# Where the first image's selective scan stands in the planner's order: in front of the scan inputs from its second direction on

## The chip, the core and the metric

The kernel runs on one core of one Trainium2 chip. The metric is device time in microseconds (us): the median of three runs before the change is 8721.23 us (8714.47 to 8724.86).

## What is computed

Four images of 64 x 64 tokens with 128 channels go through four layers: a Mamba-like block with a selective scan in four directions and an MLP (layer 0), a self attention over all 4096 tokens (layer 1), a block of convolutions (layer 2), and neighborhood attention with an MLP (layer 3). The change touches layer 0 alone. Cut to what matters there (DI = 256, N = 16, K = 4 directions, L = 4096):

```
xz = _ln(input) @ in_proj_w;  x_, z = split(xz)
xc = _silu(depthwise_conv3x3(x_) + conv_b)
xs = stack([x0, x1, x0 reversed, x1 reversed])      # row order, column order
dts, Bs, Cs = split(einsum(xs, x_proj_w))
delta = softplus(einsum(dts, dt_w) + dt_b)
h[t] = exp(delta[t] * A) * h[t-1] + (delta[t] * x[t]) * B[t]
y[t] = sum over N of h[t] * C[t]
y = the four directions added up, with Ds * xs
out = input + (_ln(y) * _silu(z)) @ out_proj_w;  then an MLP
```

## The kernel before

**The stages of an image.** `scan_inputs` (L283) makes what the scan reads: per chunk of 512 tokens the layer norm (its bn_stats and bn_aggr on VectorE, L194 and L196), the input projection, the 3 x 3 convolution on TensorE (L253), Silu on ScalarE, and then, in `steps` (L302), the projections to delta, B and C, softplus on ScalarE (L402, L403), and du = delta x xc on GpSimd (L334, two for each chunk and each order of tokens, 32 an image). All of it is stored to scratch memory: delta, B/C, sz and xc through ScalarE's queue (L331, L332, L388, L390), du through SyncE's (L338). The x loads stand on SyncE's queue too (L344). Each call opens its own pools, `si_a` and others, and closes them; the next pools that are opened lie on the same addresses and wait until the earlier ones are released.

`selective_scan` (L463) runs one image's scan: the four directions in the order 0, 1, 3, 2 (`ORDER`), eight chunks each, two halves of the channels, four groups of states and two pairs. One such step is called a unit here; an image has 512 units, 128 a direction. A unit is one product dB = du x B on GpSimd (L510), two exponentials dA on ScalarE (L516) and two scans on VectorE (L518), and then the product with C: on VectorE (L523), or, for 6 units of 16 of image 0 and 7 of 16 of the later images (`ON_POOL`), on GpSimd (L531). TensorE sums over the states (L564) into one PSUM tile `py`; ScalarE copies it out (L574, L581) and stores it. Directions 0 and 2 read what the token order by rows gives, 1 and 3 the order by columns. SyncE loads dt, du (L493), b_rows and c_rows (L503). The buffers: four each of dt, du, b_rows, c_rows and dB, three dA in PSUM, six hc.

`rest` (L1693) is everything behind the scan: `scan_output` (its weights are loaded first, w_onorm_w being the very first, then y, sz and x at L617 to L621), `layer1`, `layer2` and `layer3_attention` (last store at L1419). The layer 3 MLP of an image runs inside the next image's `scan_output`. `rest` opens its pools where those of `scan_inputs` lay.

**What sets the order.** The kernel is written in a tile framework. Each traced instruction takes a number from a running counter, `tc.cur_priority`. A planner plays the program through with its own durations and gives each engine, whenever that engine is free, the ready instruction with the lowest number; the order that comes out is fixed in the program. Waits between engines are semaphores. `network` (L1723) traces in this order: scan inputs of image 0, scan of image 0, `make_bias` (tables for layer 3), scan inputs of images 1 to 3, then, in turn, scan of image 1, rest of image 0, scan of image 2, rest of image 1, scan of image 3, rest of image 2, and rest of image 3. The scans are traced inside this block with a base of `SCAN_FIRST` = 10,000,000:

```
def priority(tc, K, base):
    kept = tc.cur_priority
    tc.cur_priority = K.next_priority.get(base, base)
    yield
    K.next_priority[base] = tc.cur_priority
    tc.cur_priority = kept
```

So a scan's numbers are above those of all scan inputs and rests: it takes what they leave. The groups of Silu and Gelu (`Together`, L101) have numbers of their own: the first of a group the highest (50 x `SCAN_FIRST`), the others and the return to the exp table the lowest (-100 x `SCAN_FIRST`).

After the scan inputs of image 3, `network` opens the pool `ss_more`, again on the addresses that scan inputs used, and calls `widen` (L452) for four more hc and one more dB tile. `Tiles.tile` (L455) counts from -40, so the first 40 tiles of image 1's scan still come from the old pool.

Of the kernel before, what the change touches and what calls it, by code (L numbers as in the profile page):

```python
# [53 lines left out]
ORDER = (0, 1, 3, 2)  # L54
BEHIND = 2
ON_POOL = ((1, 4, 6, 9, 12, 14), (0, 2, 4, 6, 9, 11, 13))
SCAN_FIRST = 10_000_000
# [20 lines left out]
@contextmanager  # L78
# [7 lines that stand above are left out]
# [42 lines left out]
def make_consts(ctx, tc):  # L128
    nc = tc.nc
    K = SimpleNamespace(next_priority={}, general=False)  # L130
    pool = ctx.enter_context(tc.tile_pool(name="consts", bufs=1))
    K.ident = pool.tile([128, 128], F32, name="ident")
    make_identity(nc, K.ident)
    K.ones = pool.tile([128, 128], F32, name="ones")
    nc.gpsimd.memset(K.ones, 1.0)
    K.mean_col = pool.tile([128, 1], F32, name="mean_col")
    nc.gpsimd.memset(K.mean_col, 1.0 / DI)
    K.mhalf = pool.tile([128, 128], F32, name="mhalf")
    nc.gpsimd.memset(K.mhalf, -0.5)
    K.half = pool.tile([128, 1], F32, name="half")  # L140
    nc.gpsimd.memset(K.half, 0.5)
    K.zeros = pool.tile([1, LC], mybir.dt.bfloat16, name="zeros")
    nc.gpsimd.memset(K.zeros, 0.0)
    K.eps = pool.tile([128, 1], F32, name="eps")
    nc.gpsimd.memset(K.eps, 1e-5)

    K.quads = pool.tile([128, 4], F32, name="quads")
    nc.gpsimd.memset(K.quads, 0.0)
    for r in range(4):
        nc.gpsimd.memset(K.quads[32 * r : 32 * r + 32, r : r + 1], 1.0)  # L150
        nc.gpsimd.memset(K.quads[32 * r : 32 * r + 1, :], 0.0)

    K.bounds = pool.tile([128, B, 8], F32, name="bounds")
    nc.gpsimd.memset(K.bounds, 0.0)

    K.first = pool.tile([128, 1], F32, name="first")
    K.first2 = pool.tile([128, 1], F32, name="first2")
    nc.gpsimd.memset(K.first, 0.0)  # L160
    nc.gpsimd.memset(K.first2, 0.0)
    for r in range(4):
        nc.gpsimd.memset(K.first[32 * r : 32 * r + 1, :], 1.0)
    for r in range(2):
        nc.gpsimd.memset(K.first2[64 * r : 64 * r + 1, :], 1.0)
    return K
# [104 lines left out]
def make_conv_diagonals(tc, K, A, out):  # L271
    nc = tc.nc
    with tc.tile_pool(name="mk_conv", bufs=1) as pool:
        convw = pool.tile([128, ND, 9], F32, name="convw")
        nc.sync.dma_start(convw, A["L0_conv_conv_w"])
        diag = pool.tile([128, ND, 9, 128], F32, name="conv_diag")
        for d in range(ND):
            for t in range(9):
                nc.scalar.activation(diag[:, d, t, :], K.ident, AF.Copy, scale=convw[:, d, t : t + 1])
        nc.sync.dma_start(out, diag)  # L280
# [135 lines left out]
def make_scan(ctx, tc, K, A):  # L416

    nc = tc.nc
    S = SimpleNamespace()
    big = ctx.enter_context(tc.tile_pool(name="ss_big", bufs=1))  # L420
    S.pool = ctx.enter_context(tc.tile_pool(name="ss", bufs=2))
    S.psum = ctx.enter_context(tc.tile_pool(name="ss_ps", bufs=1, space=PSUM))
    load = loader(tc, big, A, 0)
    S.A = load("A_log", [128, KD, NJS, NPR, 2])
    nc.scalar.activation(S.A, S.A, AF.Exp)
    nc.vector.tensor_scalar_mul(S.A, S.A, -1.0)
    ds4 = load("Ds", [128, ND, KD])
    total = big.tile([128, ND], F32, name="Dsum")
    nc.vector.tensor_reduce(total, ds4, AX.X, ALU.add)
    S.skip = big.tile([128, ND, 128], F32, name="skip_diag")  # L430
    for d in range(ND):
        nc.scalar.activation(S.skip[:, d, :], K.ident, AF.Copy, scale=total[:, d : d + 1])

    S.pick = big.tile([128, 32], F32, name="pick")
    nc.gpsimd.memset(S.pick, 1.0)
    for base, sign in ((0, 1), (3, -1)):
        nc.gpsimd.affine_select(
            S.pick, S.pick, [[-4 * sign, 32]], ALU.is_ge, 0.0, base=base, channel_multiplier=sign
        )
    S.unit = 0  # L440
    S.products = Tiles(S.pool, "hc", 6)
    S.inputs = Tiles(S.pool, "dB", 4)
    return S
# [16 lines left out]
        return pool.tile([128, 2, LC], F32, name=self.name, bufs=bufs)  # L460


def selective_scan(tc, K, S, D, img):  # L463

# [9 lines left out]
    def settle(unit):  # L476
        while waiting and waiting[0][0] <= unit:
            waiting.pop(0)[1]()

    for k in ORDER:  # L480
        back = k >= 2
        order = slice(None, None, -1) if back else slice(None)
        last = 0 if back else LC - 1
        state = pool.tile([128, NJS, NPR, 2], F32, name="state")
        for i in range(NCH):
            c = NCH - 1 - i if back else i
            for hf in range(2):
# [11 lines left out]
                for j in range(NJS):  # L499
# [85 lines left out]
                    waiting.append((max([S.unit] + [w[0] for w in waiting]), total))  # L585
                    settle(S.unit)
    settle(S.unit + BEHIND)


def scan_output(tc, K, A, D, img, xT, last, scan_over=None):  # L590
# [1132 lines left out]
def network(tc, A, out):  # L1723
    nc = tc.nc
    with ExitStack() as ctx:
        nc.scalar.preload_act_table_set("natural_log_exp_and_others")
        K = make_consts(ctx, tc)
        dram = ctx.enter_context(tc.tile_pool(name="scratch", bufs=1, space=DRAM))

        def scratch(name, shape):  # L1730
            return dram.tile(shape, F32, name=f"{name}_dram")

        D = SimpleNamespace()
        D.bias = scratch("bias", [len(BIAS_KINDS), 128, HEADS * 512])
        D.biasT = [[scratch(f"biasT{k}_{i}", [128, HEADS, LC]) for i in range(4)] for k in range(3)]
        D.T = scratch("T", [128, HEADS * (2 * KW - 1) + 1, W])
        D.conv_diag = scratch("conv_diag", [128, ND, 9, 128])
        D.w2_norms = scratch("w2_norms", [128, len(NORMS2), 4])
        D.w2_cv4, D.w2_bias = scratch("w2_cv4", [128, 128]), scratch("w2_bias", [1, 128])
        for name, shape in (("sz", [128, ND, LC]), ("xc", [128, ND, LC]), ("y", [128, ND, LC])):  # L1740
            setattr(D, name, [[scratch(f"{name}{b}_{c}", shape) for c in range(NCH)] for b in range(B)])
        for name, shape in (("delta", [128, ND, LC]), ("du", [128, ND, LC]), ("bc", [NS, 2, LC])):
            made = [
                [[scratch(f"{name}{b}_{k}_{c}", shape) for c in range(NCH)] for k in range(KD)] for b in range(B)
            ]
            setattr(D, name, made)
        D.y_first = [[[scratch(f"y_first{b}_{k}_{c}", [128, ND, LC]) for c in range(NCH)] for k in range(2)] for b in range(B)]
        D.y_cols = [scratch(f"y_cols{b}", [NCH, 128, NCH, ND, RC * RC]) for b in range(B)]
        for name in ("x4", "x5"):
            setattr(D, name, [scratch(f"{name}_{b}", [NT, C]) for b in range(B)])  # L1750
        D.shift = [scratch(f"shift{b}", [NJ, 128]) for b in range(B)]

        with ExitStack() as scan_ctx:
            S = make_scan(scan_ctx, tc, K, A)
            make_conv_diagonals(tc, K, A, D.conv_diag)
            with priority(tc, K, SCAN_FIRST // 2):
                with tc.tile_pool(name="mk_w2", bufs=1, side="right") as pool:
                    make_layer2(tc, K, A, D, pool)
            scan_inputs(tc, K, A, D, 0)
            before = None  # L1760
            for img in range(B):
                with priority(tc, K, SCAN_FIRST):
                    selective_scan(tc, K, S, D, img)
                if img == 0:
                    make_bias(tc, K, A, D)
                    for later in range(1, B):
                        scan_inputs(tc, K, A, D, later)
                    more = scan_ctx.enter_context(tc.tile_pool(name="ss_more", bufs=1))
                    S.products.widen(more, 4)
                    S.inputs.widen(more, 1)  # L1770
                else:
                    rest(tc, K, A, D, img - 1, before)
                    before = img - 1, out[img - 1]
            rest(tc, K, A, D, B - 1, before, scan_ctx.close, out[B - 1])
        needed = ctx.enter_context(tc.tile_pool(name="needed", bufs=1)).tile([1, 1], mybir.dt.int32, name="needed")
        bound_exceeded(tc, K, needed)
        with tc.If(nc.values_load(needed) > 0):
            everything_again(tc, K, A, D, out)
# [80 lines left out]
```

## Time and profile before

| what | us |
|---|---|
| median of three runs | 8721.23 |
| the profiled execution, its own time | 8724.62 |
| its span from first to last instruction | 8722.7 |
| scan inputs, first to last du product: image 0 | 79.8 to 518.7 |
| image 1 | 664.8 to 1080.7 |
| image 2 | 1166.3 to 1579.9 |
| image 3 | 1661.8 to 2084.6 |
| scan, start of the first and of the last dB product: image 0 | 101.2 to 2241.0 |
| image 1 | 2245.6 to 4049.3 |
| image 2 | 4053.9 to 5837.6 |
| image 3 | 5842.2 to 7640.4 |

The first three rows are read against each other: a sum that is made from the profile belongs to the span, and the execution that was profiled took 1.9 us more than its span. The du products show how far the scan inputs are, the dB products how far the scans are. In the profile's lines, PE is TensorE, PEld its weight loads, DVE is VectorE, ACT is ScalarE, POOL is GpSimd and SPq is SyncE's queue of DMA issues. L510 is line 510 of the kernel. A group of instructions is shown as out<-in, shapes and count, then its busy time and the mean of one in ns, then how long its engine was idle just before it and what ended that wait.

### The profile page before, as it was taken

How to read it: one execution, taken by the hardware profiler on the slowest of the kernel's cores; microseconds unless marked ns; L12 is line 12 of the kernel's file. 1: busy time of each engine (PE TensorE's matmuls, PEld its weight loads, DVE VectorE, ACT ScalarE, POOL GpSimd, SP SyncE). 2: the span in 40 equal slices, each digit the busy share in tenths (PEclk: the TensorE clock that was granted, in tenths of full speed). 3: DMA queues.
4: the chain of work that ended last, by engine and by line, in shares of the span. 5: the costliest groups of instructions: out<-in, count | busy, mean ns of one | idle time of the engine just before them, and what ended most of it. 6: DMA issues, size and time to landing. Idle time of an engine off the chain costs nothing. (4 is left out here: it accounts for less than half of the span.)

```text
span 8722.7 us, 102005 instructions
## 1 busy us (share of the span) xinstructions
PE 7011.5 (80%) x30532; PEld 2619.6 (30%) x30532; DVE 7102.0 (81%) x8456; ACT 5678.8 (65%) x11633; POOL 7121.9 (82%) x3111
## 2 busy tenths in 40 slices
PE   6858677686789987777899887777898877888988
PEld 2213122232422222233322222234322222344333
DVE  4788777778999999998899999998899999923433
ACT  5657676665666676667766676667766766654366
POOL 6899989999899989998899989998899999900000
PEclk8768687786899988888899988888999988899989
DMA  5676767677555556565555565565545565620020
GB/s 177 238 256 239 249 224 252 230 246 237 177 175 170 168 170 222 187 222 188 164 174 169 177 202 190 196 224 178 169 167 167 177 211 193 208 73 5 1 83 12
DMA packets 859600, 1562.74 MB, mean 179 GB/s; under 512 B 224389, under 2 KB 342300, under 8 KB 856733
## 3 DMA queue, kind: packets, MB, share of 16 engines
q1 hardware_dynamic: 728733, 1379.93, 48.2%
q10 hardware_dynamic: 130304, 176.19, 5.7%
q8 instruction: 245, 4.01, 0.2%
q14 instruction: 318, 2.61, 0.1%
HBM read 1286.50 MB, written 281.92 MB: 180 GB/s over the span
## 5 line engine op out<-in xcount | busy, mean ns | idle before, releaser
L510 POOL TENSOR_TENSOR dB<-du,b_rows 128x1024 f32<-128x1024 f32 x2048 | 4816.6, 2386 | 405.8 <-DVE hc L518 125.7
L516 ACT ACTIVATE dA<-dt,w_A_log 128x512 f32<-128x512 f32 x4096 | 2777.4, 690 | 482.3 <-DVE hc L518 257.7
L518 DVE TENSOR_TENSOR_SCAN dA<-dA,state,dB 128x512 f32<-128x512 f32 x2072 | 2563.4, 1274 | 289.8 <-POOL dB L510 151.8
L518 DVE TENSOR_TENSOR_SCAN hc<-dA,state,dB 128x512 f32<-128x512 f32 x1512 | 1874.1, 1270 | 303.3 <-ACT dA L516 114.2
L531 POOL TENSOR_TENSOR hc<-hc,c_rows 128x1024 f32<-128x1024 f32 x864 | 2061.9, 2386 | 60.6 <-ACT state L527 18.5
L523 DVE TENSOR_TENSOR hc<-dA,c_rows 128x512 f32<-128x512 f32 x2368 | 1526.0, 678 | 37.8 <-DMA c_rows<-bc_dram 15.2
L564 PE MATMUL py<-hc,pick 128*32 128x512 f32 x8192 | 1242.0, 681 | 266.6 <-POOL hc L531 230.9
L525 ACT COPY state<-dA 128x1 f32<-128x1 f32 x2072 | 319.2, 158 | 1225.5 <-DVE hc L523 1208.6
L854 PE MATMUL pa<-e,l_v 128*128 128x512 f32 x2048 | 1069.4, 654 | 14.9 <-ACT e L810 14.8
L810 ACT ACTIVATE e<-pair 128x1024 f32<-128x1024 f32 (+1 forms) x448 | 509.0, 1136 | 241.3 <-PE pair L806 233.7
L806 PE MATMUL pair<-l_g,l_f 32*128 32x512 f32 x2048 | 527.3, 662 | 169.6 <-ACT e L810 135.4
L854 PEld LDWEIGHTS pa<-e,l_v 128*128 128x128 f32 x2048 | 376.6, 200 | 667.1 <-issue 621.8
L994 POOL MEMSET l_h<- 64x128 f32 x8 | 1.9, 238 | 693.7 <-DVE l_h L968 693.7
L564 PEld LDWEIGHTS py<-hc,pick 128*32 128x32 f32 x8192 | 214.8, 116 | 1019.5 <-issue 476.1
L253 PE MATMUL ps<-band,w_conv_diag 128*128 128x504 f32 (+3 forms) x1152 | 499.0, 592 | 0.0
L1376 PE MATMUL pair<-table,ident 128*128 128x512 f32 x768 | 404.7, 652 | 104.2 <-ACT e L1386 68.7
L207 PE MATMUL ps<-ident,ln_xn 128*128 128x128 f32 x512 | 141.6, 375 | 377.4 <-ACT ln_xn L204 301.1
L518 DVE TENSOR_TENSOR_SCAN dA<-dA,dB 128x512 f32<-128x512 f32 x296 | 348.3, 1212 | 52.5 <-ACT dA L516 28.0
L334 POOL TENSOR_TENSOR du<-delta,xc 128x1024 f32<-128x1024 f32 x128 | 333.5, 2611 | 49.5 <-ACT delta L403 45.1
L1386 ACT ACTIVATE e<-pair 128x1024 f32<-128x1024 f32 (+1 forms) x224 | 254.3, 1135 | 101.4 <-PE pair L1380 100.7
L253 PEld LDWEIGHTS ps<-band,w_conv_diag 128*128 128x128 f32 x1152 | 220.3, 192 | 278.3 <-issue 259.7
L806 PEld LDWEIGHTS pair<-l_g,l_f 32*128 32x128 f32 x2048 | 138.4, 187 | 518.6 <-ACT e L810 266.9
(285 smaller groups left out, 8716.7 us busy)
## 6 DMA issues: line engine op xcount, KB each, us to landing
b_rows<-bc_dram SPq DMA_DIRECT2D x1024, 256.0 KB
c_rows<-bc_dram SPq DMA_DIRECT2D x1024, 256.0 KB
dt<-delta_dram SPq DMA_DIRECT2D x512, 512.0 KB
du<-du_dram SPq DMA_DIRECT2D x512, 512.0 KB
delta_dram<-delta ACTq DMA_DIRECT2D x128, 512.0 KB
du_dram<-du SPq DMA_DIRECT2D x128, 512.0 KB
table<-biasT_dram SPq DMA_DIRECT2D x72, 512.0 KB
y_first_dram<-y_sum ACTq DMA_DIRECT2D x128, 256.0 KB
```

What stands on the lines that cost most here:

```text
L253: mm = nc.tensor.matmul(out[:, r0 - row0 : r1 - row0, c0:c1], lhsT((dy + 1) * 3 + dx + 1), src[:, r0 + dy : r1 + dy, c0 + dx : c1 + dx], s ...
L334: nc.gpsimd.tensor_mul(du.rearrange("p d (a b) -> p d a b", b=H), deltas[b].rearrange("p d (a b) -> p d a b", b=H), tk,)
L510: nc.gpsimd.tensor_mul(dB, dus[pp], mid(bt, 2))
L516: nc.scalar.activation(dA, dts[pp][:, g, :], AF.Exp, scale=S.A[:, k, j, pr, g : g + 1])
L518: nc.vector.tensor_tensor_scan(hg[:, order], dA[:, order], dB[:, g, order], 0.0 if i == 0 else state[:, j, pr, g : g + 1], ALU.mult, ALU.add,)
L523: mm = nc.vector.tensor_mul(hc[:, g, :], dA, ct)
L531: made.append(nc.gpsimd.tensor_mul(hc, hc, mid(ct, 2)))
L564: mm = nc.tensor.matmul(py[0][32 * q : 32 * q + 32, :], S.pick, hcs[q // 2][:, q % 2, :], start=(k == 1 and j == 0), stop=(j == NJS - 1),)
L806: nc.tensor.matmul(ps[:, u, :], f[quad, t // 4, span(t % 4, 128)], g[quad, c, :], start=True, stop=True)
L810: made = nc.scalar.activation(e, ps, AF.Exp)
L854: nc.tensor.matmul(pa, v[:, 8 * q + t, :], es[q], start=(t == 0 and q == 0), stop=(t == 7 and q == 3),)
L1376: nc.tensor.matmul(ps[:, u, :], K.ident, t[:, u, :], start=True, stop=False)
```

## The change

`selective_scan` takes a further argument, `later`. For image 0 alone it is -`SCAN_FIRST`. When the loop over directions comes to its second one (k = 1), the counter is set to -10,000,000, and it counts on from there through directions 1, 3 and 2, so that their numbers are below those of all scan inputs, of `make_bias` and of the rests. At the end the counter is set back to where the first direction had left it, and the scans of images 1 to 3 have numbers above the inputs and rests as before. No instruction is added or taken away; the waits that come with the data and the buffers are those of the code as it stands.

```diff
-def selective_scan(tc, K, S, D, img):
+def selective_scan(tc, K, S, D, img, later=None):
...
     for k in ORDER:
+        if later is not None and k == ORDER[1]:
+            kept, tc.cur_priority = tc.cur_priority, later
         back = k >= 2
...
     settle(S.unit + BEHIND)
+    if later is not None:
+        tc.cur_priority = kept
...
                 with priority(tc, K, SCAN_FIRST):
-                    selective_scan(tc, K, S, D, img)
+                    selective_scan(tc, K, S, D, img, -SCAN_FIRST if img == 0 else None)
```

## The prediction

> **What bounds the kernel now.** I read the page's busy shares first, then one table of busy time by stage, and then SyncE's timeline at the places where one stage hands over to the next.
>
> ```profile
> PE 7011.5 (80%) x30532; PEld 2619.6 (30%) x30532; DVE 7102.0 (81%) x8456; ACT 5678.8 (65%) x11633; POOL 7121.9 (82%) x3111
> ```
>
> No engine is full over the span. By stage (columns: stretch, its length, then busy time and count of PE, weight loads, DVE, ACT, POOL, and clock, DMA share, GB/s):
>
> ```profile
> 640.00:2090.00 1450.00, 1050.83 (x3155) 356.81 (x3154) 1126.92 (x1295) 977.66 (x2196) 1349.54 (x573) 0.77 0.71 243
> 2404.00:3095.00 691.00, 623.79 (x2554) 190.10 (x2550) 656.54 (x700) 462.90 (x896) 689.54 (x299) 0.94 0.52 171
> 3290.00:3841.00 551.00, 437.27 (x2578) 164.30 (x2577) 525.01 (x588) 359.74 (x761) 551.00 (x238) 0.89 0.62 205
> 8436.00:8687.00 251.00, 216.44 (x1783) 103.09 (x1784) 96.79 (x147) 174.56 (x278) 0.00 (x0) 0.94 0.09 33
> ```
>
> The first row holds the scan inputs of images 1 to 3 with image 0's scan behind them: GpSimd idles 1450 - 1349.5 = 100.5 us. The second and third are layer 1 and layer 3 of image 0 beside image 1's scan: GpSimd is full. The last is layer 3 of image 3 with no scan beside it: 251 us for what takes 551 us beside a scan.
>
> So two chains run side by side: the scans, and the "rest" of each image (scan output, layers 1 to 3). SyncE's timeline shows how the rests are chained:
>
> ```profile
> 2087.49 0.33 SPq L338 DMA_DIRECT2D du_dram<-du  x1
> 2087.86 0.42 SPq L172 DMA_DIRECT2D w_onorm_w<-in_L_conv_onorm_w  x1
> ...
> 3854.93 0.37 SPq L1419 DMA_DIRECT2D x_dram<-x  x1
> ...
> 3859.33 0.36 SPq L172 DMA_DIRECT2D w_onorm_w<-in_L_conv_onorm_w  x1
> ...
> 7665.52 0.38 SPq L1419 DMA_DIRECT2D x_dram<-x  x1
> 7667.77 0.33 SPq L172 DMA_DIRECT2D w_onorm_w<-in_L_conv_onorm_w  x1
> ```
>
> The load of w_onorm_w is the first instruction of a rest. Rest 0 starts 0.4 us after the last du store of image 3's scan inputs, though its first y has lain in memory since 1766 (first y_dram store). It waits for the space that the scan inputs' pools hold, not for the scan. Rest 1 starts 4.4 us after rest 0's last attention store, rest 2 at 5774.0 after 5771.6, rest 3 at 7667.8 after 7665.5. The starts are 2087.9, 3859.3, 5774.0 and 7667.8; the tail is 8722.7 - 7667.8 = 1054.9 us. The scans are the other chain: the last y store is at 7651.3, 16 us before rest 3 starts. The end is therefore set by the rests, and hardly less by the scans. Whatever delays the last du store at 2087.5 delays the first chain.
>
> **The change part by part.** Nothing is added or removed: of image 0's scan, three of four directions (384 of 512 units, a unit being one dB product with its two scans) change their place in the planner's order, together with their DMAs. They go in front of image 0's remaining inputs, the bias tables and the inputs of images 1 to 3.
>
> *Cost of a unit.* These are the groups by line and shape:
>
> ```profile
> L510 POOL TENSOR_TENSOR dB<-du,b_rows 128x1024 f32<-128x1024 f32 x2048 | 4816.6, 2386 | 405.8 <-DVE hc L518 125.7 <-PE py L564 53.2 <-issue 48.7
> L531 POOL TENSOR_TENSOR hc<-hc,c_rows 128x1024 f32<-128x1024 f32 x864 | 2061.9, 2386 | 60.6 <-ACT state L527 18.5 <-issue 15.6 <-PE ps L207 7.7
> L518 DVE TENSOR_TENSOR_SCAN dA<-dA,state,dB 128x512 f32<-128x512 f32 x2072 | 2563.4, 1274 | 289.8 <-POOL dB L510 151.8 <-ACT dA L516 120.5 <-issue 7.5
> L523 DVE TENSOR_TENSOR hc<-dA,c_rows 128x512 f32<-128x512 f32 x2368 | 1526.0, 678 | 37.8 <-DMA c_rows<-bc_dram 15.2 <-PE py L564 7.3 <-PE pair L806 3.2
> ```
>
> With 6 of 16 C products on GpSimd a unit costs GpSimd 2.386 x (1 + 6/16) = 3.28 us and VectorE 2 x 1.274 + 2 x 10/16 x 0.678 = 3.40 us. In the first stage above it took 1450 us / 347 dB products = 4.18 us, as each scan input also takes du products (L334: 333.5 us / 128 = 2.61 us; 32 an image).
>
> *What is gained.* With the scan in front, GpSimd's gaps there shrink. From 93% busy to 96% (my choice, between 93% and layer 1's 99.8%) is worth some 45 us of that stage, to the scan chain alone.
>
> *What is lost.* The scan inputs give way on every engine. VectorE is full in the scan's own view (3.40 of 3.40 us), so the few bn_stats and bn_aggr of a chunk must find a hole. ScalarE gives the scan 2 x 0.69 (L516) + 0.27 (state copies, 0.158 and 0.190 each by their groups) + 0.07 (y copies, 0.583 for eight units) = 1.72 us a unit, about half its time, and each hop of the layer norm, softplus and copies can wait behind it. On SyncE's queue the x loads (L344) and du stores (L338) come behind dt, du, b_rows and c_rows loads (L493, L503), whose waits for buffers hold up what is queued after them. On ScalarE's queue the stores of sz, xc, delta and bc wait with their engine; then the du and delta buffers stay full, and the next softplus waits.
>
> No row shows scan inputs behind a scan. Bounds: at best they keep their pace; at worst they nearly stand still until the scan is over. The nearest row is the reverse, the scan as the stream behind: layer 1 lets it run at 691 us / 208 dB = 3.32 us (stage count of L510), the scan inputs at 4.18 us, so standing behind cost it a fifth of its pace. I take 0.82 of their own pace for the inputs. Above the middle, because the planner believed that GpSimd has room: in GpSimd's order 157 of image 0's 192 products stand after the dB product four units later, so all four dB buffers were full whenever a product came up, and du products get holes.
>
> *The sum.* Before, the inputs of images 1 to 3 ran from 584.8 (first x load) to 2087.5: 1503 us. From 640 on, 384 units need 384 x 3.28 = 1260 us of GpSimd. The du products take 0.82 x 96 x 2.61 / 1503 = 13.7% of it; at 96% busy the scan has 82.3% and ends 1260 / 0.823 = 1531 us later, at 2171 (before: 2241). By then the inputs have done 55 + 0.82 x 1531 = 1310 of 1503 us. The other 193 us run in front again: the last du store is at 2364, 276 us late, and so is rest 0. Meanwhile image 1's scan does 193 / 4.18 = 46 units, just what Tiles.widen lets it do before it needs the pool that lies where the inputs' pools lie. So no stall yet; at 2364 it is 12 units (some 43 us) ahead of before, and the last y store comes at about 7608.
>
> The rests keep their lengths beside a scan, so rest 2 would end at 7668 + 276 = 7944. From 7608 on no scan runs beside it: 336 us of its work left. Layer 3 alone is 551 / 251 = 2.2 times as fast, but there it also has more PSUM; I take 1.6, between 1 and 2.2. 336 / 1.6 = 210 us; it ends at 7818, 150 us late, and the tail is unchanged. The profiled execution's own 8724.6 us become 8875; its median of three is 3.4 us lower, so 8871 us.
>
> One rule speaks for the change. The Trainium skill, Perfetto Trace Analysis, sections Identifying the Most-Contended Engine and Optimization Strategy: the engine of highest occupancy is to be worked on, by closing its gaps, and regimes are to be interleaved. By it GpSimd (82%) counts and its 100.5 us of gaps are the prize: at most 8721 - 100 = 8621 us. By the handover rows the prize goes to the scan chain, which is not the later one, while the inputs, which hold up the rests, become later. I go by the rows.
>
> **The rivals.** (1) *The inputs keep pace.* GpSimd's order had room (above), so du products may slip in without delay, while about 45 us of gaps close in 640 to 2090. The last du store stays at 2087, the scans end 45 us sooner, at 7606, and rest 2's last 62 us run without a scan: 62 x (1 - 1/1.6) = 23 us, so about 8695 us. It decides if the inputs lose under some 20 us, 1.5% of their pace. For it: the room. Against: strict precedence on four engines. Faster: 0.12. (2) *The inputs starve.* VectorE's order has no holes for bn_stats. At half pace the scan ends at 640 + 1260 / 0.876 = 2078, the inputs still lack 729 us; image 1's scan stops after 46 units (193 us) for want of its pool, and the remaining 536 us, faster without a scan (by 1.3, say), end at about 2683. GpSimd idles, the scans end near 7930, rest 2 near 8140: some 9190 us. 0.18. (3) *Nothing moves*: image 0's second direction gets its buffers only as before, or the inputs' loss is eaten by the rests' overlap. 8721 us, 0.10.
>
> **How the numbers follow.** My case, the inputs late by 100 to 450 us and the end by 40 to 280 us, has 0.60; its own range is 8760 to 9000. A measurement tells about 0.2% (17 us) from no change. Faster 0.12 (rival 1), same 0.10 (rival 3), slower 0.60 + 0.18 = 0.78. The range reaches down to rival 1 (8690) and up into rival 2, to 9090, which leaves out about 0.12 above and 0.05 below.
>
> **What would show it.** In the changed profile: image 0's 512th dB product well before 2241 (my step: 2171); the last du store of the fourth image well after 2087 (2364) with w_onorm_w right behind it; GpSimd above 93% until the scan's end; the four rest starts shifted by one amount, the last by less. A last du store at 2090, or a rest 0 that starts before it, would prove me wrong; GpSimd empty after 2100 would be rival 2.

## The result and the profile after

The changed kernel takes 8813.14 us (median of five, 8806.34 to 8817.05), the one before 8721.23; the ratio is 1.0106, 95% interval 1.0094 to 1.0117. The loss is 92 us. The profiled execution took 8809.4 us, with a span of 8807.5 us, 84.8 us more than before.

The busy shares of the changed kernel say next to nothing. GpSimd and VectorE do the same work in a longer span:

```profile
PE 7048.9 (80%) x30532; PEld 2635.5 (30%) x30532; DVE 7093.4 (81%) x8456; ACT 5678.7 (64%) x11633; POOL 7121.2 (81%) x3111
```

The table by stage of the changed kernel (columns as in the prediction) shows where the change did what it was meant to do. From 640 until the inputs are done GpSimd is 1423 / 1486 = 95.8% busy, after 93.1%. The fourth row is the stretch from the end of the scans' last dB product to rest 3, where GpSimd is almost empty (the scans' last y store comes at 7634.4):

```profile
640.00:2126.00 1486.00, 1075.81 (x3258) 364.47 (x3254) 1196.44 (x1371) 1014.63 (x2283) 1423.07 (x604) 0.77 0.71 246
2448.00:3132.00 684.00, 615.79 (x2516) 187.62 (x2514) 641.86 (x683) 451.57 (x860) 672.01 (x291) 0.94 0.52 172
6308.00:7004.00 696.00, 621.32 (x2537) 188.82 (x2536) 657.83 (x698) 465.06 (x893) 691.34 (x300) 0.93 0.52 173
7626.00:7750.00 124.00, 98.49 (x606) 41.99 (x598) 10.38 (x21) 30.51 (x43) 4.84 (x3) 0.89 0.14 46
```

SyncE's timeline of the changed kernel, at the handovers that were shown of before (start, duration, queue, line, transfer):

```profile
2123.40 3.14 SPq L338 DMA_DIRECT2D du_dram<-du  x2
2126.59 0.42 SPq L172 DMA_DIRECT2D w_onorm_w<-in_L_conv_onorm_w  x1
...
3916.90 0.36 SPq L1423 DMA_DIRECT2D x_dram<-x  x1
3921.76 0.36 SPq L172 DMA_DIRECT2D w_onorm_w<-in_L_conv_onorm_w  x1
...
5833.86 0.36 SPq L1423 DMA_DIRECT2D x_dram<-x  x1
5836.57 0.36 SPq L172 DMA_DIRECT2D w_onorm_w<-in_L_conv_onorm_w  x1
...
7748.13 0.37 SPq L1423 DMA_DIRECT2D x_dram<-x  x1
7750.54 0.35 SPq L172 DMA_DIRECT2D w_onorm_w<-in_L_conv_onorm_w  x1
```

Rest 0 again starts within half a microsecond of the last du store, now at 2126.6 instead of 2087.9. The later rests start 62.5, 62.6 and 82.7 us later than before. So of the 84.8 us, 38.7 are there when rest 0 starts, 24 more come in rest 0, none in rest 1, 20 in rest 2, and 2 in the tail. The scans went the other way: image 0's last dB product starts at 2181 (before 2241), image 3's at 7623.8 (before 7640.4), so a lead of 60 us had shrunk to 17. The end came later although every scan ended sooner.

### The profile page after: what moved, and what is told of

Its sections match the earlier page's. It is cut to its first block, busy times and chain, and to the rows that moved or that the text cites. A ratio compares the mean times of both kernels' runs of the same rounds, so it can differ in the third digit from the quotient of the medians.

```text
span 8807.5 us, 102036 instructions
## 1 busy us (share of the span) xinstructions
PE 7048.9 (80%) x30532; PEld 2635.5 (30%) x30532; DVE 7093.4 (81%) x8456; ACT 5678.7 (64%) x11633; POOL 7121.2 (81%) x3111
## 5 line engine op out<-in xcount | busy, mean ns | idle before, releaser
L512 POOL TENSOR_TENSOR dB<-du,b_rows 128x1024 f32<-128x1024 f32 x2048 | 4871.3, 2448 | 391.7 <-DVE hc L520 90.5
L533 POOL TENSOR_TENSOR hc<-hc,c_rows 128x1024 f32<-128x1024 f32 x864 | 2117.5, 2451 | 59.3 <-issue 23.8
L566 PE MATMUL py<-hc,pick 128*32 128x512 f32 x8192 | 1222.8, 675 | 229.6 <-POOL hc L533 206.8
```

The lines of the kernel that those rows point to most:

```text
L512: nc.gpsimd.tensor_mul(dB, dus[pp], mid(bt, 2))
L533: made.append(nc.gpsimd.tensor_mul(hc, hc, mid(ct, 2)))
L566: mm = nc.tensor.matmul(py[0][32 * q : 32 * q + 32, :], S.pick, hcs[q // 2][:, q % 2, :], start=(k == 1 and j == 0), stop=(j == NJS - 1),)
```

## The experiments

Each median stands beside runs of the kernel before on the same chip, which gave 8721.8 (e1 to e4), 8720.5 (e5 to e8) and 8718.8 us (e9 to e12); the ratios are to these. The starts are those of one profiled execution of each kernel, which for e1, e6 and e8 took 9 to 10 us more than the median. "Rest 0" and "rest 3" are the starts of the first loads of these rests in the trace; "scans" is the start of image 3's last dB product; "three rests" is rest 3 less rest 0.

| kernel | rest 0 | scans | rest 3 | three rests | median | ratio, 95% interval |
|---|---|---|---|---|---|---|
| before | 2087.9 | 7640.4 | 7667.8 | 5579.9 | 8721.2 | 1 |
| the change | 2126.6 | 7623.8 | 7750.5 | 5623.9 | 8813.1 | 1.0106, 1.0094 to 1.0117 |
| e1, fourth direction | 2085.4 | 7630.2 | 7664.4 | 5579.0 | 8715.7 | 0.9992, 0.9983 to 1.0000 |
| e2, third and fourth | 2124.9 | 7612.6 | 7695.3 | 5570.4 | 8758.3 | 1.0047, 1.0033 to 1.0061 |
| e3, all four | 2188.3 | 7624.7 | 7742.6 | 5554.3 | 8794.4 | 1.0081, 1.0067 to 1.0095 |
| e4, longer inputs | 2157.0 | 7662.5 | 7767.9 | 5610.9 | 8823.0 | 1.0120, 1.0104 to 1.0135 |
| e5, change + copies, image 1 | 2111.8 | 7600.2 | 7679.3 | 5567.5 | 8735.1 | 1.0018, 1.0011 to 1.0025 |
| e6, before + copies, image 1 | 2092.3 | 7644.6 | 7671.9 | 5579.6 | 8720.9 | 0.9999, 0.9991 to 1.0008 |
| e7, image 3's inputs in front | 2111.9 | 7604.3 | 7687.5 | 5575.6 | 8747.4 | 1.0035, 1.0022 to 1.0049 |
| e8, du on VectorE | 2079.1 | 7645.6 | 7670.2 | 5591.1 | 8723.3 | 1.0005, 0.9996 to 1.0013 |
| e9, change + copies, image 2 | 2125.4 | 7615.8 | 7743.0 | 5617.6 | 8802.6 | 1.0102, 1.0087 to 1.0117 |
| e10, change + copies, image 3 | 2129.0 | 7623.3 | 7750.0 | 5621.0 | 8806.5 | 1.0103, 1.0087 to 1.0118 |
| e11, e4 + copies, image 2 | 2153.3 | 7662.9 | 7768.4 | 5615.1 | 8825.9 | 1.0120, 1.0105 to 1.0136 |
| e12, image 0 without GpSimd's C products | 2029.3 | 7444.8 | 7595.8 | 5566.5 | 8653.8 | 0.9926, 0.9912 to 0.9939 |

The theory: the rests decide, rest 0's start is the term that the change moves, and it hangs on the last du store of image 3's inputs. The rival: the scans (GpSimd's work) decide, and the loss is the planner's other reshuffling.

### The dose: how much of the scan stands in front (e1, e2, e3)

```diff
-        if later is not None and k == ORDER[1]:
+        if later is not None and k == ORDER[3]:     # e1; ORDER[2] in e2, ORDER[0] in e3
```

Expected of e1: 

> Only the fourth direction of image 0's scan (128 of 512 units) goes in front. Theory (the end follows the last du store of image 3's inputs, which opens rest 0): only the inputs of image 3 run behind a scan, so that store comes 10 to 25 us after 2087 and the end 15 to 45 us after the kernel before: 8735 to 8765 us. Rival (the loss comes from the planner's other reshuffling, the end has no tie to that store): no order between the one and the other, a time anywhere between 8700 and 8815.

Expected of e2: 

> The third and fourth directions of image 0's scan (256 units) go in front. Theory: last du store 20 to 35 us later than 2087, end 30 to 70 us later than before: 8750 to 8790 us, between the fourth alone and the change. Rival: no order among the four doses.

Expected of e3: 

> All four directions of image 0's scan go in front, so image 0's own inputs stand behind it as well. Theory: last du store 50 to 80 us later than 2087, end 90 to 150 us later than before: 8810 to 8870 us. Rival: the scan has the most precedence here and ends earliest, so the end is no later than with the change, 8720 to 8813 us.

Measured: e1 missed its range from below. The inputs lost nothing (rest 0 at 2085.4), the scans ended 10 us sooner, and the time is 6 us lower, inside what this kernel's measurement can tell from none. The end of e2 fell into its range, with rest 0 at +37 just above the expected 20 to 35. e3 missed the theory's range (8810 to 8870) and lies in the rival's: it ended at 8794, less than the 8813 of the change; its rest 0 started 100 us late, more than the expected 50 to 80, while its end moved by 73. The start of rest 0 grows with the dose (-2, +37, +39, +100 us), which is the theory's. The end does not follow one to one (-6, +37, +92, +73): the three rests differ by up to 70 us. e2 and the change start rest 0 within 2 us of each other and end 55 us apart, so the late start alone does not make the change's 92 us. One of three doses kept its forecast: this series supports the start of rest 0, not the size of the end.

### Lateness alone (e4)

```diff
         for c in range(NCH):
             steps(1, c)
+        if img == B - 1:
+            for _ in range(4):
+                steps(1, NCH - 1)
```

> The kernel before, order of priorities untouched; image 3's inputs do the last column step four times more (the same values written again), which makes only the inputs longer: some 17 us a step. It adds 8 du products, 21 us of GpSimd. Theory: rest 0 starts 60 to 75 us later and the end moves by as much or up to half more: 8780 to 8830 us. Rival (GpSimd's work and the scans decide): only the added 21 us show, 8735 to 8750 us.

No priority is changed here. SyncE's timeline of e4:

```profile
2156.60 0.33 SPq L338 DMA_DIRECT2D du_dram<-du  x1
2156.97 0.42 SPq L172 DMA_DIRECT2D w_onorm_w<-in_L_conv_onorm_w  x1
...
7765.47 0.37 SPq L1422 DMA_DIRECT2D x_dram<-x  x1
7767.88 0.35 SPq L172 DMA_DIRECT2D w_onorm_w<-in_L_conv_onorm_w  x1
```

Rest 0 starts 69 us late, rest 3 100 us late, the end is 101 us late: the theory's range, and far from the rival's 8735 to 8750. Inputs that end late suffice for most of a loss of this size, with 21 us more of GpSimd's work: 69 of the 101 us are the late start, 31 are rests that grew, here without any change of priority.

### The opposite: scans much sooner (e12)

```diff
-                        if on_pool:
+                        if on_pool and img == 0:
+                            made.append(scanned)
+                        elif on_pool:
```

(`scanned` is the scan instruction.)

> The kernel before without the C products that GpSimd does for image 0: for 6 units of 16 of that image the states are summed without C, which takes 192 x 2.36 = 453 us of work from GpSimd and gives nothing to another engine. If the scans' chain decides, image 0's scan ends some 300 us sooner and the end falls by 250 us or more (under 8470). If the handover decides, rest 0 still starts between 2050 and 2090, image 1's scan gets ahead, and the end falls by the part of rest 2 that then runs alone and the slip of rest 0: 60 to 180 us, 8540 to 8660 us.

```profile
2028.78 0.45 SPq L338 DMA_DIRECT2D du_dram<-du  x1
2029.28 0.86 SPq L172 DMA_DIRECT2D w_onorm_w<-in_L_conv_onorm_w  x1
...
7593.40 0.37 SPq L1421 DMA_DIRECT2D x_dram<-x  x1
7595.81 0.34 SPq L172 DMA_DIRECT2D w_onorm_w<-in_L_conv_onorm_w  x1
```

The scans end 196 us sooner, yet the end falls by 65 us, 0.74%, inside the range of the handover: about what rest 0's start fell by (59 us, to 2029; 2050 to 2090 was expected). Here the two chains come apart widest, and the end goes with the rests. This also weighs the rule of the Trainium skill (Perfetto Trace Analysis, Identifying the Most-Contended Engine) that the prediction set against the rows: 453 us taken from the engine of highest occupancy brought 65 us, and those by way of the inputs.

### Image 3's inputs back in front (e7)

```diff
                     for later in range(1, B):
-                        scan_inputs(tc, K, A, D, later)
+                        if later == B - 1:
+                            with priority(tc, K, -2 * SCAN_FIRST):
+                                scan_inputs(tc, K, A, D, later)
+                        else:
+                            scan_inputs(tc, K, A, D, later)
```

> The change, but image 3's inputs stand in front of image 0's scan. Theory (rest 0's start is a term of the end): image 3's inputs take some 505 us again instead of 525, rest 0 starts 15 to 25 us earlier (2102 to 2112), and the end falls by as much, with the layout's 20 to 40 us on top: 8750 to 8815 us. Rival (scan precedence is what cost): nothing gained, as the scan loses precedence just where the change had given it: 8813 or later.

Rest 0 started at 2111.9, inside the expected 2102 to 2112, 15 us sooner than with the change, and the end fell by 66 us, 3 below the range. From image 2's last du store to image 3's it is 507 us instead of 525. The direction is the theory's; the size is not: the three rests lost 48 us as well.

### Is the rest of the loss an accident of layout? (e5, e6, e9, e10, e11)

```diff
         state = pool.tile([128, NJS, NPR, 2], F32, name="state")
+        if img == 1:                                # 2 in e9 and e11, 3 in e10
+            nc.scalar.copy(state[:, 0, 0, :], K.ident[:, 0:2])
```

Expected of e5, on the change: 

> The change as it is, plus four tiny copies on ScalarE (one at each direction of image 1's scan, 0.16 us each, overwritten before they are read), which make the planner lay out everything behind them anew. Rest 0's start cannot move by more than a few us (2127). If the 44 us that the three rests gained with the change are an accident of the planner's layout, their sum (5624 us) falls back toward 5580 or moves by 20 us or more, and the end lies 20 to 60 us below 8813. If they belong to the change, the sum stays within 10 us and the end at 8803 to 8823 us.

Expected of e6, on the kernel before: 

> The same four tiny copies in the kernel before. If the layout is an accident of some 20 to 40 us, the sum of the three rests (5580 us) moves by as much with rest 0 starting at 2088 as before: 8690 to 8760 us. If layouts are stable, 8712 to 8732 us.

Expected of e9, on the change: 

> The change, with the four tiny copies in image 2's scan instead of image 1's, so that what the planner lays out before it (all inputs, image 1's scan, most of rest 0) should stay: rest 0 starts at 2127 again. If the 44 us by which the three rests grew are an accident of layout, their sum leaves 5624 by 20 us or more, most likely downward, and the end comes to 8740 to 8800 us; if they belong to the late start, 8803 to 8823 us.

Expected of e10, on the change: 

> The same with the copies in image 3's scan: rest 0 and rest 1 should stay (starts 2127, 3922, 5837), only rest 2 beside image 3's scan is laid out anew. Accident of layout: rest 2's length leaves 1914 us by 10 to 40 us and the end moves with it, 8770 to 8830; no accident: 8803 to 8823 us.

Expected of e11, on e4: 

> The kernel with four more input steps of image 3 (rest 0 at 2157, end 8823) with the four tiny copies in image 2's scan. Rest 0's 69 us stay. If layout made the other 31 us, the end falls by 10 to 60 us, to 8765 to 8815, and never below 8750, as the late start remains; if they belong to the late start, 8813 to 8833 us.

Measured: e5 fell by 78 us, to 8735, more than the 20 to 60 expected. Rest 0, which was not to move, came 15 us sooner, and the three rests were 56 us shorter. The first of its copies (0.19 us) stands at 1682, among image 3's inputs. So much can one small instruction move. But e6, with the same copies in the kernel before, moved nothing, though its first copy stands among image 3's inputs too (1723). Nor did e9, e10 and e11, whose copies run from 3550, 5382 and 3602 on: the rests stayed as they were within 7 us. So the expectation that any disturbance would shuffle the rests was wrong. The 44 us of the three rests are stable against copies behind the inputs; they are not bound to a late start of rest 0 (e2 has it without them), and a layout changed among the inputs can lose them (e5, e7).

Where they lie can be read. Cut each rest at its first load, at the first and last exponential of layer 1 on ScalarE and at the first of layer 3, and add up the three rests (us):

| kernel | scan output | layer 1 | layer 2 | layer 3 | three rests |
|---|---|---|---|---|---|
| before | 1229 | 2007 | 641 | 1704 | 5580 |
| the change | 1261 | 2038 | 634 | 1691 | 5624 |
| e2 | 1206 | 2042 | 637 | 1686 | 5570 |
| e7 | 1228 | 2046 | 627 | 1676 | 5576 |

Against the kernel before, scan output and layer 1 grew by 32 us each. But e2 and e7 have a layer 1 as long as the change's. What sets the change apart from e2, which starts rest 0 at the same time, is the scan output: 55 us.

Layer 1 and scan output of image 2 beside image 3's scan: the first two rows are the kernel before, the third is the changed kernel's scan output (its layer 1 is the third row of its stage table above):

```profile
6230.00:6883.00 653.00, 600.85 (x2471) 181.20 (x2472) 620.16 (x659) 442.35 (x837) 648.60 (x281) 0.95 0.52 173
...
5774.00:6229.80 455.80, 336.56 (x1386) 169.57 (x1386) 395.37 (x544) 324.76 (x722) 378.32 (x163) 0.83 0.57 182
...
5836.60:6308.70 472.10, 344.75 (x1384) 170.67 (x1384) 396.40 (x542) 326.69 (x736) 377.70 (x163) 0.82 0.53 172
```

Layer 1 took 653 us with 281 GpSimd instructions before, 696 us with 300 after: 2.32 us for each in both, with GpSimd 99% busy. A longer layer could have let more of them in; but the order on ScalarE is fixed in the program, and between the first and last exponential of this layer it holds 395 exponentials of the scan before and 422 after, 1.65 us for each in both. So the planner put more of the scan into this layer, and the layer is longer for it. In image 1's layer 1 it put fewer (396 instead of 409; 656 us instead of 676). The scan output does not follow the count: 163 GpSimd instructions both times, 456 us before and 472 after, with GpSimd idle for 77 and 94 us. What it waits for there, and which difference in the planner's order makes it, stays open.

### du on VectorE (e8)

```diff
-                nc.gpsimd.tensor_mul(
+                (nc.gpsimd if img == 0 else nc.vector).tensor_mul(
                     du.rearrange("p d (a b) -> p d a b", b=H),
```

> The kernel before with the du products of images 1 to 3 on VectorE: 96 x 2.61 = 251 us less for GpSimd between 640 and 2090, some 96 x 1.36 = 130 us more for VectorE (twice the 0.678 us of a half as wide product). If GpSimd's total decides, the end falls by 150 to 250 us: 8470 to 8570. If the handover decides, image 0's scan ends 80 to 170 us sooner, but the last du store comes only 10 to 60 us sooner, and the end falls by that and by the part of rest 2 that runs without a scan: 30 to 110 us, 8610 to 8690.

```profile
640.00:2090.00 1450.00, 1050.72 (x3142) 357.69 (x3146) 1325.39 (x1383) 970.05 (x2184) 1178.31 (x476) 0.77 0.71 241
...
L334 DVE TENSOR_TENSOR du<-delta,xc 128x1024 f32<-128x1024 f32 x96 | 224.4, 2344 | 3.2 <-ACT delta L403 1.7 <-ACT state L525 1.5
```

(The first line is e8's busy time in that stage, the second its group of du products on VectorE.) Both ranges were missed: 8723 us, the same as before. A du product on VectorE took 2344 ns on average, not the 1360 that I had reckoned, as most of them stood still while GpSimd worked (last section). So VectorE got 224 us for GpSimd's 251 and was 91% busy, and GpSimd's busy time fell by 171 us only; image 0's scan ended at 2246, as before. Rest 0 came 9 us sooner and the three rests were 11 us longer. This run exchanged one nearly full engine for another and does not tell the theories apart; e12 does that.

## Why the prediction was right, and where not

- **What bounds it.** Right: rest 0 hangs on the last du store (0.4 to 0.5 us between them in all 14 kernels), and the end goes with the rests and not with the scans (e4, e12).
- **The gain.** Right in place and size: GpSimd went from 93% to 95.8% (96% was taken), image 0's scan ended at 2181 (2171), 60 us sooner, and all of it stayed in the scans' chain. Of the lead, 43 us were to reach the last y store (7608); 17 did (7634 after 7651).
- **The loss of the inputs.** The mechanism is right, its size was not. "I take 0.82 of their own pace for the inputs" is the term: from their first x load to their last du store they took 1543 us (582.8 to 2126.2) instead of 1503, a pace of 0.974, so rest 0 came 39 us late and not 276. The reason given for the slowness, "VectorE is full in the scan's own view", does not hold in the profile: VectorE was 1196 / 1486 = 80.5% busy there, and 1127 / 1450 = 78% in the first row of the prediction's own table. The row the pace was taken from, a scan behind inputs, says nothing of inputs behind a scan: the "fifth of its pace" is for the most part GpSimd's time for the du products themselves, 250 / 1450 = 17%, which the inputs' place in the order does not change. The reason given for a higher pace, the room in GpSimd's order, fits what came; no run isolates it.
- **What was to come back.** "The rests keep their lengths beside a scan" failed: they grew by 44 us, against a predicted relief of 126. The last start was to shift by less than the others; it shifted by the most (82.7 us). The relief exists, as far as two other images can stand for the same layer: after the scans ended, 124 us of rest 2 ran alone, and its layer 3 with the wait for rest 3 took 580 us where images 0 and 1 took 624 and 625; 456 + 124 k = 625 gives a factor k of 1.36 (1.6 was taken). The longer scan outputs and layers 1 spent it. The predicted 126 also counts the 16 us that rest 2 ran alone before (7651 to 7668); without them it is 120, and rival 1's 23 us are 17.
- **The sum.** 276 less 126 was to give 150; it became 39 + 44 + 2 = 85 in the profile, 92 in the medians. Two terms that were wrong stood against each other, the lateness too large by 237 us and a relief where there was a loss; that 8871 lies so near 8813 is luck. What is shown: about half of the loss is the late handover; the other half lies in the rests' layout, located in scan output and layer 1 but not traced to its cause.
- **The rivals.** Rival 1 (inputs keep pace) decides under 20 us of lateness; with 39 us it was near, and e1, with the last direction alone in front, is that case: lateness -2 us, time 6 us lower, which is not clear of noise. It had 23 us to win, but with 45 us of lead for the scans; in e1 they ended 10 us sooner. Rival 2 (starved inputs) is refuted: VectorE had holes, and from 2100 to 2180 GpSimd was 71 of 80 us busy.

No kernel here that does all the work beats the one before clear of noise; e1 comes nearest. e12 is faster, but leaves work out.

## What to carry to other kernels

Where stages share memory, look in the queue's timeline for the first load of the next stage and the last store of the one whose space it takes: that pair, not the busiest engine, says what may be put behind what. Work that stands last in trace order can still hold up the chain that ends last. And where a planner interleaves two streams and the engine that paces one of them is full, as in layer 1 here, count that stream's instructions inside a stage before taking the stage's length as given.

## What the runs showed of the hardware

VectorE and GpSimd took turns in e8, where VectorE made the du products (f32, both inputs in SBUF) beside GpSimd's products. Three instructions of its trace:

```profile
1396.48 2.36 POOL L510 TENSOR_TENSOR dB<-du,b_rows 128x1024 f32<-128x1024 f32 x1
...
1396.55 3.37 DVE L334 TENSOR_TENSOR du<-delta,xc 128x1024 f32<-128x1024 f32 x1
...
1400.44 1.21 DVE L334 TENSOR_TENSOR du<-delta,xc 128x1024 f32<-128x1024 f32 x1
```

The second du product ran with GpSimd idle and took 1.21 us. The first began 0.07 us after a GpSimd product and ended 1.08 us after that one's end, 3.37 us in all. So it is throughout: 20 of the 96 du products began while no GpSimd product ran, and took 1.2 us (token order by rows) or 1.9 us (by columns); the others ended 1.1 or 1.8 us after the GpSimd product that they had met, with one exception. The other way round, the 112 GpSimd products that overlapped a du product took 3.00 us on average, the 364 others in that stretch 2.36. The C product on VectorE, which has one of its inputs in PSUM, took 677 ns for 512 elements beside the same GpSimd and 678 before: it does not wait, and the du product alone is no slower for each element. The Trainium skill, SBUF — State Buffer, section Who interferes with whom, says that a VectorE instruction with two SBUF inputs and a GpSimd instruction that reads SBUF exclude each other; this trace agrees.
